# Selective scan: the product with C as one instruction per group on GpSimd, the product with B split unevenly between VectorE and GpSimd

## The chip, the cores and the metric

The kernel runs on one core of a Trainium2 chip. The metric is the device time of one execution in microseconds; the time of a kernel is the median of several executions. The core has five engines that work side by side, each through its own queue in order: TensorE (PE in the profile) multiplies matrices, VectorE (DVE) and GpSimd (POOL) work elementwise, ScalarE (ACT) applies functions such as exp, and SyncE (SP) here issues the transfers (DMA). They wait for each other through semaphores.

## The reference, cut to what matters

The program is a chain of four layers on an input of 2 images, 128 channels, 64 x 64 pixels: an attention layer, a layer of deformable convolutions, a layer of residual convolutions, and a layer of four selective scans. Only the last is touched. For each image, each of four directions (by rows forward and backward, by columns forward and backward) is a sequence of 4096 steps with 256 inner channels d and 16 states n:

```
dt  = softplus(dt @ W_dt.T + b_dt)
dA  = exp(dt[..., None] * A)                       # decay
dBu = dt[..., None] * Bm[:, :, None, :] * xh[..., None]
def step(h, inp):
    dA_t, dBu_t = inp
    h = dA_t * h + dBu_t
    return (h, h)
_, hs = lax.scan(step, h0, (dA.transpose(1, 0, 2, 3), dBu.transpose(1, 0, 2, 3)))
y = jnp.einsum('lbdn,bln->bld', hs, Cm)            # product with C, sum over n
y = y + xh * Dp
y = y * jax.nn.silu(z)
```

The four directions' results are joined, projected and added to the input.

## The kernel before, in words

Layer 3 is the function `layer3` (from line 1103). A sequence is cut into blocks of BLK = 512 steps: 2 images x 4 directions x 8 blocks make 64 blocks. In each block the 256 channels are two halves (`hf`), and the 16 states are four sets of four (`ng`). A half and a set make a group, so that a block has eight groups, numbered in this text 0 to 7 (4 x hf + ng), and the loop runs over 512 groups. In a group the 128 partitions hold 4 states x 32 channels, and four parts (`q`) of 512 steps each hold the half's four sets of 32 channels. The work of a group k:

- `weights` (line 1347): a matmul spreads the four rows of B over the partitions, into PSUM (tile `pbc`).
- `db_dve` (line 1361, VectorE) multiplies this B with dt times u (tile `dd4`, its second plane) for the first ND = 3 of the four parts; `db_pool` (line 1368, GpSimd) does the fourth, with a copy of B that a DMA has spread in SBUF[...]. Both write the tile `db`, of which there are four buffers.
- `expo` (line 1375, ScalarE): exp for the decay, one part at a time, into a PSUM tile `da` of which there are three; it runs two parts ahead of the scan.
- `scan` (line 1384, VectorE): one scan instruction for each part, in place in `db`.
- `keep` (line 1390, ScalarE) saves the last column of two parts to start the next block from.
- `cmul` (line 1395, GpSimd) multiplies two parts with C (also a copy spread by DMA), in place.
- `sums` (lines 1401 and 1403, PE) adds over the states into PSUM; after group 3 and group 7 of a block, `gate` (line 1412, VectorE) multiplies the sum with silu(z).

The order of all this is written out by hand in the loop that starts at line 1544; every engine takes its instructions in this order. In iteration k, VectorE has the four scans of group k, sometimes a gate, then `db_dve` of group k+1. GpSimd has `db_pool` of k+1, the second half of `cmul` of k-1, then the first half of `cmul` of k. ScalarE runs the decays, and between them the front work of the next block, spread over the iterations of the present one (`front_act`): in iteration 0 the silu that makes u, between two loads of its function table; 1 copies; 2 and 3 softplus; 4 a copy and `finish`; 5 the silu of z, again between two table loads. GpSimd has two small products of the next block's delta work in iterations 3 and 4 (`spread`). PE has that front work's matmuls ahead of `sums`. `transfers` puts the DMAs into SP's queue: storing and spreading delta (`spread_store`, `spread_load`, lines 1331 and 1340) and the copies of B and C (`copies`, line 1355).

Of the kernel before, what the change touches and what calls it, by code (L numbers as in the profile page):

```python
# [20 lines left out]
P = 128  # L21
# [3 lines left out]
BLK = 512  # L25
# [1077 lines left out]
def layer3(g, I, out):  # L1103
# [4 lines left out]

    nc, tc = g.nc, g.tc
    NJ = 4  # L1110
    ND = 3
    NNG = N_STATE // NJ
    HB = 3
    with ExitStack() as ctx:
# [66 lines left out]
        hl = a.tile([P, 2, NNG, 4, 1], F32, name="hl")  # L1181
# [58 lines left out]
        S = {}  # L1240
# [15 lines left out]
        def conv(i, hf):  # L1256
            blk = blocks[i]
            sgn = -1 if dirs[blk[1]][2] else 1
            pu = S[i]["pu", hf] = psm.tile([P, BLK], F32, name="pm3")
            for s in range(4):  # L1260
                nc.tensor.matmul(shaped(blk, pu), wcs[:, hf, s, :], window(blk, sgn * s), start=(s == 0), stop=(s == 3))  # L1261
# [33 lines left out]
        def bc_store(i):  # L1295
            S[i]["bx"] = dr.tile([2 * N_STATE, BLK], F32, name="bx")
            nc.sync.dma_start(S[i]["bx"], S[i]["xd"][: 2 * N_STATE])
# [30 lines left out]
        def spread_store(i, hf):  # L1328

            S[i]["dx", hf] = dr.tile([P, 2, BLK], F32, name="dx")  # L1330
            nc.sync.dma_start(S[i]["dx", hf], S[i].pop(("dd", hf)))

        def spread_load(i, hf):
            s_ = S[i]
            dx = s_.pop(("dx", hf))
            dd4 = d4.tile([P, 2, 4, BLK], F32, name="dd4")
            for x in range(2):
                src = dx[:, x, :].rearrange("(q c) t -> c q t", c=32)
                for j in range(NJ):
                    nc.sync.dma_start(dd4[32 * j : 32 * j + 32, x], src)  # L1340
            s_["d4", hf] = dd4

        def weights(k):

            i, hf, ng = groups[k]
            pb = psb.tile([P, BLK], F32, name="pbc")
            nc.tensor.matmul(pb, sel[:, ng].rearrange("p j c -> p (j c)"), S[i]["bc"], start=True, stop=True)  # L1347
            G[k] = {"pb": pb}

        def copies(i, x, ng):  # L1350

            t = S[i][x, ng] = ck.tile([P, BLK], F32, name=f"{x}4_{ng}", bufs=1)
            r0 = NJ * ng + (N_STATE if x == "c" else 0)
            for j in range(NJ):
                nc.sync.dma_start(t[32 * j : 32 * j + 32], S[i]["bx"][r0 + j].partition_broadcast(32))

        def db_dve(k):
            i, hf, ng = groups[k]
            x, n = G[k], ND
            x["db"] = wk.tile([P, 4, BLK], F32, name="db")  # L1360
            nc.vector.tensor_tensor(  # L1361
                x["db"][:, :n, :], x.pop("pb").unsqueeze(1).to_broadcast([P, n, BLK]), S[i]["d4", hf][:, 1, :n, :], ALU.mult
            )

        def db_pool(k):
            i, hf, ng = groups[k]
            x, n = G[k], ND
            nc.gpsimd.tensor_tensor(  # L1368
                x["db"][:, n:, :], S[i]["b", ng].unsqueeze(1).to_broadcast([P, 4 - n, BLK]), S[i]["d4", hf][:, 1, n:, :], ALU.mult
            )  # L1370
# [12 lines left out]
            first = i % NBLK == 0  # L1383
            nc.vector.tensor_tensor_scan(d1, d0, d1, 0.0 if first else hl[:, hf, ng, q, :], ALU.mult, ALU.add)  # L1384

        def keep(k, h):
            i, hf, ng = groups[k]
            last = 0 if dirs[blocks[i][1]][2] else BLK - 1
            qs = slice(2 * h, 2 * h + 2)
            nc.scalar.copy(hl[:, hf, ng, qs], G[k]["db"][:, qs, last : last + 1])  # L1390

        def cmul(k, h):
            i, hf, ng = groups[k]
            v = G[k]["db"][:, 2 * h : 2 * h + 2, :]
            nc.gpsimd.tensor_mul(v, v, S[i]["c", ng].unsqueeze(1).to_broadcast([P, 2, BLK]))  # L1395

        def sums(k):
            i, hf, ng = groups[k]
# [10 lines left out]
        def gate(i, hf):  # L1409
            s_ = S[i]  # L1410
            gt = s_["gt", hf] = ck.tile([P, BLK], F32, name="gt")
            nc.vector.tensor_tensor(gt, s_.pop(("y", hf)), s_["z"][:, hf, :], ALU.mult)  # L1412
# [24 lines left out]
        G = {}  # L1437

        def begin(i):
            if i < NBK:  # L1440
                S[i] = {}
                if i % (4 * NBLK) == 0:
                    columns_halo(blocks[i][0])
                if i % (4 * NBLK) == 2 * NBLK:
                    rows_halo(blocks[i][0])
                conv(i, 0)
# [3 lines left out]
        def front_act(i, slot):  # L1450
            if i < NBK:
                if slot == 0:
                    conv_silu(i)
                elif slot == 1:
                    xproj_copy(i)
                elif slot == 2:
                    softplus(i, 0)
                elif slot == 3:
                    softplus(i, 1)
                elif slot == 4:  # L1460
                    rest_copy(i)
                elif slot == 5:
                    zproj_silu(i)
# [18 lines left out]
        def front_pe(i, slot):  # L1482
            if i < NBK:
                if slot == 1:
                    xproj(i)
                elif slot == 2:
                    delta(i, 0)
                elif slot == 3:
                    delta(i, 1)
                elif slot == 4:  # L1490
                    xproj_rest(i)
                elif slot == 5:
                    zproj(i)
            if i + 1 < NBK:
                if slot == 6:
                    begin(i + 1)
                elif slot == 7:
                    conv(i + 1, 1)

        def front_pool(i, slot):  # L1500
            if i < NBK:
                if slot in (3, 4):
                    spread(i, slot - 3)
# [11 lines left out]
        with tc.manual_schedule():  # L1515
            tc.keep_in_program_order(nc.scalar.preload_act_table_set("natural_log_exp_and_others"))
            nc.scalar.activation(am, am, AF.Exp)
            nc.vector.tensor_scalar(am, am, -1.0, None, ALU.mult)
            for t in range(NBLK + 1):
                for s in LN:  # L1520
                    if 0 <= t - s // 8 < NBLK:
                        LN[s](0, t - s // 8)
            begin(0)
            conv(0, 1)
            for slot in range(8):
                front_pe(0, slot)
                front_act(0, slot)
                front_pool(0, slot)
            bc_store(0)
            for hf in range(2):  # L1530
                spread_store(0, hf)
            spread_load(0, 0)
            for ng in range(NNG):
                copies(0, "b", ng)
                copies(0, "c", ng)
            weights(0)
            weights(1)
            db_dve(0)
            db_pool(0)
            units = [(k, q) for k in range(len(groups)) for q in range(4)]  # L1540
            AHEAD = 2
            for u in range(AHEAD):
                expo(*units[u])
            for k in range(len(groups) + 6):
                i, slot = divmod(k, 8)
                live = k < len(groups)
                more = k + 1 < len(groups)
                ended = 1 <= k <= len(groups)
                transfers(i + 1, slot)
                if k + 2 < len(groups):  # L1550
                    weights(k + 2)
                for q in range(4):
                    if 4 * k + q + AHEAD < len(units):
                        expo(*units[4 * k + q + AHEAD])
                    if q == 0 and ended:
                        keep(k - 1, 1)
                    if live:
                        scan(k, q)

                    for j, hf in (((k - 5) // 8, 0), ((k - 9) // 8, 1)):  # L1560
                        if q == 3 and 8 * j + 5 + 4 * hf == k and 0 <= j < NBK:
                            gate(j, hf)

                    if q == 2 and live:
                        keep(k, 0)
                if more:
                    db_dve(k + 1)
                    db_pool(k + 1)
                if ended:
                    cmul(k - 1, 1)  # L1570
                front_pe(i + 1, slot)
                front_act(i + 1, slot)
                front_pool(i + 1, slot)
                if i >= 1 and i <= NBK:
                    if slot == 3:
                        project(i - 1)
                    elif slot == 4:
                        finish(i - 1)
                if live:
                    next_norm(i, slot)  # L1580
                if live:
                    cmul(k, 0)
                if ended:
                    sums(k - 1)

# [159 lines left out]
```

## Time and profile before

| | |
|---|---|
| median of 3 runs | 6007.57 us (5999.1 to 6009.02) |
| the profiled execution's own time | 6003.65 us |
| its span | 6001.9 us |
| busy in the span: PE | 5221.0 us (87%) |
| VectorE | 4554.2 us (76%) |
| ScalarE | 3807.3 us (63%) |
| GpSimd | 3701.6 us (62%) |
| first scan, last scan of layer 3 start at | 2554.8 us, 5990.1 us |

Shares over the whole span mix four layers. GpSimd is hardly used before 2500 us and almost without a pause after it, so the stage has to be read by itself. In a row of the profile's groups stand: line, engine, operation, tile written and tiles read, shapes and count; then the busy time in us and the mean ns of one; then the idle time of the engine just before these instructions, and what ended most of it.

### The profile page before, as it was taken

The numbers are of one execution on the slowest core, as the hardware profiler recorded it, in microseconds if no ns is written. First come the engines' busy times: TensorE is split into PE (matmuls) and PEld (weight loads), VectorE is DVE, ScalarE is ACT, GpSimd is POOL, SyncE is SP. The second block draws the span as 40 slices with busy tenths as digits, with TensorE's granted clock in tenths as the row PEclk, the third lists the DMA queues.
The fourth block names the chain that finished last, engine by engine and source line by source line (L and its number), as shares of the span: only waits on it lengthen the run. The fifth ranks groups of instructions, "written<-read, shape, count | busy, mean of one in ns | idle before, by whom it ended". The sixth has DMA issues, their size and how long they took to land.

```text
span 6001.9 us, 60094 instructions
## 1 busy us (share of the span) xinstructions
PE 5221.0 (87%) x18726; PEld 1662.7 (28%) x18726; DVE 4554.2 (76%) x4262; ACT 3807.3 (63%) x5867; POOL 3701.6 (62%) x2108
## 2 busy tenths in 40 slices
PE   6999999989978689888998888888898888887877
PEld 3333333334444334212222222222222222222221
DVE  5333333355134698499999999999999999999999
ACT  3888888840035411377777766777777777777765
POOL 5111111100010121199999999999999999999999
PEclk9999999999988899888888888888888888888887
DMA  5000001020066200165665556655665556655564
GB/s 152 18 18 18 18 18 32 1 58 1 15 111 110 51 7 0 28 144 135 145 144 133 138 134 145 143 131 135 150 145 132 141 132 145 145 134 137 135 151 106
DMA packets 373049, 575.61 MB, mean 96 GB/s; under 512 B 91080, under 2 KB 145744, under 8 KB 371632
## 3 DMA queue, kind: packets, MB, share of 16 engines
q1 hardware_dynamic: 367408, 563.94, 40.6%
q10 hardware_dynamic: 5312, 7.76, 0.5%
q8 instruction: 149, 2.44, 0.2%
q14 instruction: 180, 1.47, 0.1%
HBM read 482.34 MB, written 89.13 MB: 95 GB/s over the span
## 4 chain that ended last, share of the span: by engine, by line
DVE 45%; PE 38%; DMA 4%; issue 4%; POOL 4%; ACT 2%; SPq 2%; DVEq 0%; ACTq 0%; POOLq 0%
DVE db L1384 31%; DVE db L1361 11%; PE ps L269 10%; PE acc L285 8%; PE m L1034 5%; PE m L548 4%; DMA dd<-dx 2%; POOL db L1395 2%; PE acd L794 2%; PE pm L1261 1%; PE m L508 1%; DVE gt L1412 1%; PE pf L757 1%; PE py L1403 1%; PE pc L645 1%
## 5 line engine op out<-in xcount | busy, mean ns | idle before, releaser
L1395 POOL TENSOR_TENSOR db<-db,c 128x1024 f32<-128x1024 f32 x1024 | 2401.0, 2360 | 80.7 <-ACT hl L1390 67.5
L1384 DVE TENSOR_TENSOR_SCAN db<-da,hl,db 128x512 f32<-128x512 f32 x1792 | 2158.2, 1265 | 53.8 <-ACT da L1375 7.3
L1375 ACT ACTIVATE da<-dd,am 128x512 f32<-128x512 f32 x2048 | 1406.7, 689 | 918.0 <-DVE db L1384 904.0
L275 ACT ACTIVATE e<-ps 128x1024 f16<-128x1024 f32 x1024 | 992.3, 1021 | 134.8 <-PE ps L269 117.7
L1403 PE MATMUL py<-db,fold 128*32 128x512 f32 x4096 | 831.0, 686 | 203.4 <-POOL db L1395 202.9
L1361 DVE TENSOR_TENSOR db<-pbc,dd 128x1536 f32<-128x1536 f32 x512 | 888.2, 1735 | 51.1 <-DMA c<-bx 51.1
L1261 PE MATMUL pm<-xn,wcs 128*128 128x512 f32 x1024 | 722.8, 857 | 30.6 <-DVE xc L1199 17.6
L296 DVE RECIPROCAL rec<-acc 32x512 f32<-32x512 f32 x64 | 214.9, 3358 | 639.6 <-PE acc L285 612.1
L303 POOL TENSOR_TENSOR parts<-parts 32x512 f32<-32x512 f32 x64 | 80.6, 1259 | 975.3 <-DVE parts L302 975.3
L1368 POOL TENSOR_TENSOR db<-b,dd 128x512 f32<-128x512 f32 x512 | 651.2, 1272 | 21.1 <-DMA c<-bx 14.9
L269 PE MATMUL ps<-q,k 32*128 32x512 f32 x4096 | 656.4, 643 | 3.6 <-DVE flag L232 2.8
L285 PE MATMUL acc<-e,v 128*128 128x512 f16 x2048 | 531.3, 382 | 0.0
L1034 PE MATMUL m<-v,u 128*128 128x512 f32 x864 | 376.4, 598 | 51.6 <-DVE v L1003 51.6
L1401 PE MATMUL py<-u,ddp 128*128 128x512 f32 x256 | 183.6, 806 | 232.1 <-DVE gt L1412 231.8
L1347 PE MATMUL pbc<-bc,sel 64*128 64x512 f32 x512 | 284.2, 555 | 83.7 <-DVE db L1361 77.5
L1403 PEld LDWEIGHTS py<-db,fold 128*32 128x32 f32 x4096 | 115.1, 113 | 805.2 <-POOL db L1395 517.5
L1261 PEld LDWEIGHTS pm<-xn,wcs 128*128 128x128 f32 x1024 | 203.6, 209 | 428.8 <-issue 375.8
L1384 DVE TENSOR_TENSOR_SCAN db<-da,db 128x512 f32<-128x512 f32 x256 | 293.3, 1205 | 9.0 <-ACT da L1375 0.7
L285 PEld LDWEIGHTS <-v 128*128 128x128 bf16 x2048 | 158.5, 97 | 510.0 <-issue 388.7
L269 PEld LDWEIGHTS ps<-q,k 32*128 32x128 f32 x4096 | 229.7, 183 | 228.0 <-issue 147.2
L1347 PEld LDWEIGHTS pbc<-bc,sel 64*128 64x128 f32 x512 | 104.8, 205 | 607.6 <-DVE db L1361 306.3
L548 PE MATMUL m<-comb,w 64*128 64x512 f32 (+4 forms) x1296 | 269.9, 575 | 0.0
(311 smaller groups left out, 5734.9 us busy)
## 6 DMA issues: line engine op xcount, KB each, us to landing
dd<-dx SPq DMA_DIRECT2D x1024, 256.0 KB, 6.6
dx<-dd SPq DMA_DIRECT2D x128, 512.0 KB, 7.2
b<-bx SPq DMA_DIRECT2D x1024, 64.0 KB, 5.3
c<-bx SPq DMA_DIRECT2D x1024, 64.0 KB, 2.1
hats<-pos SPq DMA_DIRECT2D x136, 256.0 KB, 9.8
q<-qd SPq DMA_DIRECT2D x32, 512.0 KB, 8.6
w<-in_conv0T SPq DMA_DIRECT2D x18, 288.0 KB, 8.8
xa<-in_x SPq DMA_DIRECT2D x8, 512.0 KB, 9.1
```

Of the source, the lines that this page charges most:

```text
L269: nc.tensor.matmul(ps[:, i, :], k4[h % 2][rows, kb // 4, :], q4[h % 2][rows, qb * BLK : (qb + 1) * BLK], start=True, stop=True,)
L275: nc.scalar.activation(e[:, :n, :], ps[:, :n, :], AF.Exp)
L285: nc.tensor.matmul(acc, v3[b][:, kb, h, :], e[:, i, :], start=(kb == 0), stop=(kb == NS - 1))
L548: yield lambda q=q, dy=dy, src=src, i0=i0, i1=i1: nc.tensor.matmul(m[:, i0 * NF : i1 * NF], w[half, dy, q, x, :], src, start=(dy == KC and ...
L1034: nc.tensor.matmul(m[x], weights[j][:, dy, x, :], v[j][b][:, x, r0 : r0 + RP, :].rearrange("p r i -> p (r i)"), start=(dy == 0), stop=(dy ...
L1261: nc.tensor.matmul(shaped(blk, pu), wcs[:, hf, s, :], window(blk, sgn * s), start=(s == 0), stop=(s == 3))
L1361: nc.vector.tensor_tensor(x["db"][:, :n, :], x.pop("pb").unsqueeze(1).to_broadcast([P, n, BLK]), S[i]["d4", hf][:, 1, :n, :], ALU.mult)
L1368: nc.gpsimd.tensor_tensor(x["db"][:, n:, :], S[i]["b", ng].unsqueeze(1).to_broadcast([P, 4 - n, BLK]), S[i]["d4", hf][:, 1, n:, :], ALU.mult)
L1375: nc.scalar.activation(da, S[i]["d4", hf][:, 0, q, :], AF.Exp, scale=am[:, hf, q, ng : ng + 1])
L1384: nc.vector.tensor_tensor_scan(d1, d0, d1, 0.0 if first else hl[:, hf, ng, q, :], ALU.mult, ALU.add)
L1395: nc.gpsimd.tensor_mul(v, v, S[i]["c", ng].unsqueeze(1).to_broadcast([P, 2, BLK]))
L1403: nc.tensor.matmul(S[i]["y", hf][32 * q : 32 * q + 32, :], fold, G[k]["db"][:, q, :], start=False, stop=(ng == NNG - 1),)
```

## The change

The number of parts that VectorE multiplies with B now depends on half and set: (2, 4, 2, 4) in the first half, (2, 4, 1, 4) in the second. Where VectorE has all four, `db_pool` issues nothing, and the spread copies of B for sets 1 and 3 are no longer transferred. GpSimd's product with C is one instruction for the four parts of a group. It stands where the second half stood, one iteration after the group's scans; the first half at the end of the group's own iteration is gone. The last columns are likewise saved in one copy for the four parts, where the second copy stood.

```diff
@@ layer3 @@
-    ND = 3
+
+    ND = ((2, 4, 2, 4), (2, 4, 1, 4))
...
         def copies(i, x, ng):
 
+            if x == "b" and ND[0][ng] == ND[1][ng] == 4:
+                return
             t = S[i][x, ng] = ck.tile([P, BLK], F32, name=f"{x}4_{ng}", bufs=1)
...
         def db_dve(k):
             i, hf, ng = groups[k]
-            x, n = G[k], ND
+            x, n = G[k], ND[hf][ng]
...
         def db_pool(k):
             i, hf, ng = groups[k]
-            x, n = G[k], ND
+            x, n = G[k], ND[hf][ng]
+            if n == 4:
+                return
...
-        def keep(k, h):
+        def keep(k):
             i, hf, ng = groups[k]
             last = 0 if dirs[blocks[i][1]][2] else BLK - 1
-            qs = slice(2 * h, 2 * h + 2)
-            nc.scalar.copy(hl[:, hf, ng, qs], G[k]["db"][:, qs, last : last + 1])
-
-        def cmul(k, h):
+            nc.scalar.copy(hl[:, hf, ng], G[k]["db"][:, :, last : last + 1])
+
+        def cmul(k):
             i, hf, ng = groups[k]
-            v = G[k]["db"][:, 2 * h : 2 * h + 2, :]
-            nc.gpsimd.tensor_mul(v, v, S[i]["c", ng].unsqueeze(1).to_broadcast([P, 2, BLK]))
+            v = G[k]["db"]
+            nc.gpsimd.tensor_mul(v, v, S[i]["c", ng].unsqueeze(1).to_broadcast([P, 4, BLK]))
...
                     if q == 0 and ended:
-                        keep(k - 1, 1)
+                        keep(k - 1)
                     if live:
                         scan(k, q)
...
-                    if q == 2 and live:
-                        keep(k, 0)
                 if more:
                     db_dve(k + 1)
                     db_pool(k + 1)
                 if ended:
-                    cmul(k - 1, 1)
+                    cmul(k - 1)
...
                 if live:
                     next_norm(i, slot)
-                if live:
-                    cmul(k, 0)
                 if ended:
                     sums(k - 1)
```

## The prediction

> **What bounds the kernel now.** I read the busy times by stage first. The scan of layer 3 runs from 2554.8 to 5991.4 us, 64 blocks of 53.7 us. Two of its stretches (columns: length, then busy us of PE, weight loads, VectorE, ScalarE and GpSimd, then clock, DMA share, GB/s):
>
> ```profile
> 3000.00:3500.00 500.00, 435.74 (x1080) 105.80 (x1079) 492.04 (x394) 357.71 (x640) 487.73 (x266) 0.86 0.58 138
> 4500.00:5000.00 500.00, 440.87 (x1066) 102.68 (x1066) 491.80 (x393) 356.41 (x638) 485.62 (x262) 0.88 0.57 136
> ```
>
> VectorE is busy 98.4%, GpSimd 97%. The groups of the page give the pieces:
>
> ```profile
> L1395 POOL TENSOR_TENSOR db<-db,c 128x1024 f32<-128x1024 f32 x1024 | 2401.0, 2360 | 80.7 <-ACT hl L1390 67.5
> L1384 DVE TENSOR_TENSOR_SCAN db<-da,hl,db 128x512 f32<-128x512 f32 x1792 | 2158.2, 1265 | 53.8 <-ACT da L1375 7.3
> L1361 DVE TENSOR_TENSOR db<-pbc,dd 128x1536 f32<-128x1536 f32 x512 | 888.2, 1735 | 51.1 <-DMA c<-bx 51.1
> L1368 POOL TENSOR_TENSOR db<-b,dd 128x512 f32<-128x512 f32 x512 | 651.2, 1272 | 21.1 <-DMA c<-bx 14.9
> ```
>
> GpSimd's idle time is mostly for the copy of last columns (line 1390); VectorE's 51.1 us is one wait, before the first group. What VectorE waits for inside the scan stands in the waits by engine:
>
> ```profile
> DVE db L1384 <- ACT da L1375: 8.0, 11, 3.2
> ```
>
> Eight us in all. VectorE therefore sets the block time; whatever it saves counts, and whatever makes it wait costs. To see what is close behind, I follow one block in the timeline. I number a block's groups 0 to 7 (half hf, then ng) and call iteration s the loop pass with group s's scans. VectorE, around iterations 5 and 6 (start, duration, instruction):
>
> ```profile
> 3604.19 4.81 DVE L1384 TENSOR_TENSOR_SCAN db<-da,hl,db 128x512 f32<-128x512 f32 x4
> 3608.92 0.66 DVE L1412 TENSOR_TENSOR gt<-py,z 128x512 f32<-128x512 f32 x1
> 3609.50 1.75 DVE L1361 TENSOR_TENSOR db<-pbc,dd 128x1536 f32<-128x1536 f32 x1
> 3611.35 4.81 DVE L1384 TENSOR_TENSOR_SCAN db<-da,hl,db 128x512 f32<-128x512 f32 x4
> ```
>
> A scan takes 1.18 us from start to start; product and gap before the next scan take 1.85. ScalarE in the same time:
>
> ```profile
> 3607.86 0.69 ACT L1375 ACTIVATE da<-dd,am 128x512 f32<-128x512 f32 x1 [0.37 <-DVE db L1384]
> 3608.57 1.28 ACT L1279 ACT_TABLE_LOAD   x1
> 3609.86 1.09 ACT L1279 ACTIVATE z<-pm 128x512 f32<-128x512 f32 x2
> 3610.97 1.28 ACT L1280 ACT_TABLE_LOAD   x1
> 3612.26 0.69 ACT L1375 ACTIVATE da<-dd,am 128x512 f32<-128x512 f32 x1
> ```
>
> The decay of group 6's third scan waits behind the block of z work and is ready at 3612.95; about 0.05 us later a scan can use it, at 3613.00. VectorE gets there at 3611.35 + 2 x 1.18 = 3613.71. The margin is 0.71 us. I measured it so in 57 blocks: 0.70 to 0.72 in 50, 0.54 to 0.65 in 7. The same reading after the u work in iteration 0 gives a margin of about -0.07 in most blocks: there VectorE already loses 0.07 us.
>
> **What the Trainium skill says.** "Perfetto Trace Analysis", Tensor Engine Instruction: ScalarE, VectorE and GpSimd run strictly in order. The trace agrees: the decay above starts when the table load ends. "ScalarE: Activation LUTs", What ACT_TABLE_LOAD costs: a load takes about 1283 ns whatever the set; the trace shows 1283, so this block of work cannot shrink. "VectorE: DVE Perf Modes", The DRAIN you can't avoid: a same-engine read after write needs a semaphore; here 0.11 us pass between each product and its first scan, and the number of such pairs stays. Price: "GPSIMD Engine Reference", 3.1, gives 4497 ns on GpSimd and 2293 on VectorE for a two-input fp32 tensor_tensor of 2048 elements.
>
> **The change part by part** (per block, then x64).
>
> *Products with B on VectorE.* Before 8 x 3 = 24 parts; after 2+4+2+4+2+4+1+4 = 23, in the same eight instructions. The gate row (512 elements, also PSUM x SBUF) has 665 ns, the 1536-element row 1735: 535 a part and 130 fixed. So 1, 2 and 4 parts cost 0.665, 1.20 and 2.27 us. Saved: 0.535 x 64 = 34.2 us. With the page's 2293 for 2048 the saving is 6 us less; 6 either way goes into the range.
>
> *Cover taken from ScalarE.* In iteration 5 VectorE goes on to group 6, which has one part: it reaches the third scan 1.735 - 0.665 = 1.07 us earlier. Of that 0.71 is margin, 0.36 becomes a wait. ScalarE's block starts by the end of scan (5,2) and does not move. Over 63 blocks with z work: 55 x 0.36 + 8 x 0.45 (the smaller margins of a direction's first blocks) = 23.4 us lost. Group 1 gets four parts, which adds 0.535 in iteration 0 and removes that wait: 45 x 0.07, and 3 us of longer waits on decays in the trace: 6 us gained. Iteration 3 (second softplus) leads to group 4 with two parts: margin 1.45 falls to 0.92; a few blocks had 0.0 to 0.6, for which I add 1 us. Iteration 1: 3.53 falls to 3.0; iteration 7: at least 0.96 falls to 0.43.
>
> *GpSimd.* The 1024 product takes 2.33 us from start to start, the 512 one 1.23: 1.10 a part. Whole product with C: 1.10 x 4 + 0.13 = 4.53 (page: 4.50; two halves now: 4.66). Products with B: three of two parts (2.33) and one of three (3.42), 10.4 against 8 x 1.23 = 9.8. Before 8 x 4.66 + 9.8 + 5.2 (delta work) = 52.3; after 36.2 + 10.4 + 5.2 = 51.8 of a block of some 53.5. It stays under VectorE. Its whole product can now start only after the last scan and the copy. Walking through its queue from the start of a block, with ScalarE's copies at their present distance from the scans: product 0 may start at 9.06 us, ends 13.6; product 1 18.1; B-product for group 4, then product 2 21.2 to 25.7; delta work 28.3; product 3 32.9; delta 35.4; the three-part B-product 38.9; product 4 43.4, product 5 47.9; B-product for the next group 0 50.2; product 6 54.8, product 7 59.3 = 5.8 of the next block; B-product 8.1, before 9.06. So it catches up once a block. Who waits for it: scan (6,1) for the three-part product, due at 41.2, 2.4 us after; the gates after product 3 and 7, 4.7 and 5 us after PE's sums; the db buffers (four), over 5 us. No wait reaches VectorE. PE's z matmuls, behind sum 3, end at 36.8, ScalarE wants them at 38.25.
>
> *Copies of B for ng 1 and 3.* 512 transfers of 64 KB and 0.43 us of the SP queue each go. SP's waits are for delta work (853.9 us), and VectorE waits for no such transfer: 0. If this cover were gone, the relief could only help. Delta work ends 2 us later in the block (28.3 against 26.3); stored and loaded as now, its half lands at about 44.5, wanted at 47.9.
>
> *Copies of last columns* (line 1390): 512 fewer of 0.18 us on a ScalarE that waits 0.37 us beside them: 0.
>
> *The end.* The last product with C is 4.53 instead of 2.33 us after the last scan: +2.2, and some 0.3 for the sums: +2.5.
>
> Sum: -34.2 + 23.4 - 6 + 1 + 2.5 = -13.3 us. The profiled execution took 6003.65 (span 6001.9): 5990.4. The median of the three runs is 6007.57; the same difference gives **5994 us**.
>
> **Rivals.**
> *A, the gain comes whole:* ScalarE is ready for the third scan. For: the margin of 0.71 is read with a start latency seen only in the u case. Against: it is the same in 50 blocks. -34.2 - 6 + 2.5 = -38 us: 5970.
> *B, slower: GpSimd becomes the bound.* Place: the whole product with C, a form that the trace doesn't show. It decides from (53.5 - 15.6) / 8 = 4.74 us each. At 4.80 a block takes 54.0, 0.5 more: +32 on the forecast, 6026. For: two halves take 4.66 already. Against: the slope of the two forms and the page.
> *C, no difference:* GpSimd's product 3 ends over 1.4 us later than in my walk, PE's z matmuls follow, and ScalarE's block moves right: each us is a us of VectorE's wait. At 0.2 us a block the gain is gone: 6007. For: PE's clock is 0.83 to 0.88 and ScalarE already waits for PE in iteration 4. Against: margins of 1.4 us.
>
> **Chances.** Forecast 0.60, A 0.10, B 0.12, C 0.18. A measurement of this kernel tells about 0.2% (12 us) from no change. The forecast's own range is 5985 to 6003, its centre barely beyond that bound: 0.36 of its 0.60 faster, 0.24 the same. With A: faster 0.46. C with 0.01 of B: same 0.42, a little of C counting as slower; slower 0.12. The range takes in A and C, and B up to 4.78 us a product: 5968 to 6015.
>
> **What would show it.** Products of VectorE at 0.67, 1.20 and 2.27 us; GpSimd's at 4.53; a wait of VectorE for the decay (line of the exponent) once a block, before group 6's third scan, some 0.36 us each and 23 in all; none in iteration 0; block time 53.5 us. Wrong it would be if GpSimd is busy over 99% or VectorE waits on products of GpSimd or on gates.

## The result, and the profile after

The changed kernel takes 6044.84 us (median; 6041.86 to 6050.66) against 6005.65 us for the kernel before: ratio 1.0068, 95% interval 1.005 to 1.0085. It is slower by 39 us where 12 to 13 us less was forecast. The profiled execution's span is 6040.1 us, 38.2 more than before.

The groups of the page for the four kinds of instruction that were shown of before:

```profile
L1399 POOL TENSOR_TENSOR db<-db,c 128x2048 f32<-128x2048 f32 x512 | 2311.0, 4528 | 58.5 <-ACT hl L1394 57.9
L1389 DVE TENSOR_TENSOR_SCAN db<-da,hl,db 128x512 f32<-128x512 f32 x1792 | 2162.7, 1265 | 113.2 <-ACT da L1380 66.3
L1364 DVE TENSOR_TENSOR db<-pbc,dd 128x2048 f32<-128x2048 f32 (+2 forms) x512 | 854.8, 1670 | 51.1 <-DMA c<-bx 51.1
L1373 POOL TENSOR_TENSOR db<-b,dd 128x1024 f32<-128x1024 f32 (+1 forms) x256 | 673.7, 2632 | 136.2 <-DMA c<-bx 86.6
```

The instructions cost what was expected: 4528 ns for the whole product with C, and VectorE's products are 33 us shorter in all (888.2 to 854.8). The time went into waits: the idle time before the scans rose from 54 to 113 us. The busy times of the same two stretches of the scan, columns as before:

```profile
3000.00:3500.00 500.00, 406.01 (x1054) 102.93 (x1056) 476.89 (x386) 339.84 (x550) 471.55 (x149) 0.84 0.52 125
4500.00:5000.00 500.00, 421.89 (x1039) 103.47 (x1043) 472.22 (x380) 336.31 (x542) 462.79 (x145) 0.83 0.53 125
```

VectorE falls from 98.4% to about 95%, GpSimd from 97% to 93 or 94%: neither is busy throughout, so neither sets the block time by its work alone. The waits by engine, over the scan of layer 3 (from 2554 us on), name the next link, VectorE's first, then ScalarE's:

```profile
DVE db L1389 <- ACT da L1380: 76.3, 93, 3.7
```

```profile
ACT u L1267 <- PE pm L1262: 72.6, 30, 4.1
```

VectorE waits 76 us for the decay, in 93 places. In 63 of them it waits before group 6's third scan, as forecast, 17 us in all (23 forecast); in the other 30 before group 1's third scan, 59 us, which the prediction does not have. ScalarE waits 72.6 us in 30 places for line 1262, a convolution of the next block's front work. Before, this was 3.6 us.

**Where the blocks differ.** I took the time from one start of group 0's product on VectorE to the next. In the row directions (blocks 16 to 31 and 48 to 63) an ordinary block takes 53.50 us (53.74 before), as forecast. In the column directions (0 to 15 and 32 to 47) the median is 55.17. By classes of these distances, after minus before: 30 of column directions +50.4 us, 24 of row directions -5.4, the 8 with layer norm (in which the second image is normalized) -5.4, the first -0.2. They sum to 39.4 us. The rest of the 38.2 us between the two spans lies outside: the first of these products starts 5.5 us earlier, after layers that the change doesn't touch, and from the last one to the end 4.4 us more pass. VectorE's timeline in a row block:

```profile
3626.80 0.67 DVE L1416 TENSOR_TENSOR gt<-py,z 128x512 f32<-128x512 f32 x1
3627.38 0.68 DVE L1364 TENSOR_TENSOR db<-pbc,dd 128x512 f32<-128x512 f32 x1
3628.17 2.46 DVE L1389 TENSOR_TENSOR_SCAN db<-da,hl,db 128x512 f32<-128x512 f32 x2
3630.87 2.46 DVE L1389 TENSOR_TENSOR_SCAN db<-da,hl,db 128x512 f32<-128x512 f32 x2 [0.25 <-ACT da L1380]
```

That is the forecast wait before group 6's third scan. In a column block there is another, in iteration 1, before group 1's third scan (VectorE, then ScalarE, then PE, then GpSimd, all around the same block's end):

```profile
2774.48 2.46 DVE L1389 TENSOR_TENSOR_SCAN db<-da,hl,db 128x512 f32<-128x512 f32 x2
2778.48 2.46 DVE L1389 TENSOR_TENSOR_SCAN db<-da,hl,db 128x512 f32<-128x512 f32 x2 [1.54 <-ACT da L1380]
```

```profile
2773.06 0.69 ACT L1267 ACTIVATE u<-pm,vecs 128x512 f32<-128x512 f32 x1
2775.75 0.69 ACT L1267 ACTIVATE u<-pm,vecs 128x512 f32<-128x512 f32 x1 [2.01 <-PE pm L1262]
2776.46 1.28 ACT L1268 ACT_TABLE_LOAD   x1
2777.76 0.69 ACT L1380 ACTIVATE da<-dd,am 128x512 f32<-128x512 f32 x1
```

```profile
2757.45 1.93 PE L1407 MATMUL py<-db,fold 128*32 128x512 f32 x8 [3.06 <-POOL db L1399]
2759.31 0.79 PE L1348 MATMUL pbc<-bc,sel 64*128 64x512 f32 x1
2760.04 7.21 PE L1262 MATMUL pm<-xn,wcs 128*128 128x512 f32 x8
2767.18 1.06 PE L1407 MATMUL py<-db,fold 128*32 128x512 f32 x8
2768.18 0.49 PE L1348 MATMUL pbc<-bc,sel 64*128 64x512 f32 x1
2768.60 7.12 PE L1262 MATMUL pm<-xn,wcs 128*128 128x512 f32 x8
```

```profile
2752.89 9.01 POOL L1399 TENSOR_TENSOR db<-db,c 128x2048 f32<-128x2048 f32 x2
2776.88 2.36 POOL L1373 TENSOR_TENSOR db<-b,dd 128x1024 f32<-128x1024 f32 x1 [3.63 <-DMA c<-bx]
```

Read backwards: the third scan waits for a decay, which stands behind the u work; u's second half waits for the second convolution, which ends at about 2775.7; the two convolutions take 7.1 us each and stand in PE's queue behind the sums of group 4, which wait until GpSimd has ended product 4 with C at 2757.40. Before, in the same block, these sums began 2.7 us earlier, and the second convolution ended 2.7 us earlier, though the next block began at nearly the same time (2766.24 us then, 2766.09 now):

```profile
2754.74 2.21 PE L1403 MATMUL py<-db,fold 128*32 128x512 f32 x8
2756.89 0.63 PE L1347 MATMUL pbc<-bc,sel 64*128 64x512 f32 x1
2757.45 7.12 PE L1261 MATMUL pm<-xn,wcs 128*128 128x512 f32 x8
2764.49 1.06 PE L1403 MATMUL py<-db,fold 128*32 128x512 f32 x8
2765.49 0.49 PE L1347 MATMUL pbc<-bc,sel 64*128 64x512 f32 x1
2765.91 7.12 PE L1261 MATMUL pm<-xn,wcs 128*128 128x512 f32 x8
```

The first theory from this: a ring. GpSimd's late products delay the convolutions, and the sums of group 6 behind the second convolution release the buffer that GpSimd needs for group 2 (the 3.63 us above, which the profile puts down to a transfer). There are two rivals: PE is merely late, and nothing comes back to GpSimd (the one-way theory); or the transfer that the profile names is late (the transfer theory).

### The profile page after: what moved, and what is told of

Same layout as the page of the kernel before. It is cut to its first block, busy times and chain, and to the rows that moved or that the text cites. A ratio compares the mean times of both kernels' runs of the same rounds, so it can differ in the third digit from the quotient of the medians.

```text
span 6040.1 us, 57348 instructions
## 1 busy us (share of the span) xinstructions
PE 5093.3 (84%) x18726; PEld 1660.5 (27%) x18726; DVE 4525.1 (75%) x4262; ACT 3749.8 (62%) x5355; POOL 3658.3 (61%) x1340
## 4 chain that ended last, share of the span: by engine, by line
PE 46%; DVE 27%; POOL 12%; ACT 5%; issue 5%; DMA 4%; SPq 1%; DVEq 0%; POOLq 0%; ACTq 0%
DVE db L1389 19%; PE ps L269 10%; PE acc L285 8%; PE pm L1262 7%; DVE db L1364 7%; POOL db L1399 7%; PE m L1034 5%; PE m L548 4%; POOL db L1373 2%; PE py L1407 2%; PE acd L794 2%; ACT da L1380 1%; PE m L508 1%; POOL dd L1326 1%; DMA dd<-dx 1%
## 5 line engine op out<-in xcount | busy, mean ns | idle before, releaser
L1399 POOL TENSOR_TENSOR db<-db,c 128x2048 f32<-128x2048 f32 x512 | 2311.0, 4528 | 58.5 <-ACT hl L1394 57.9
L1407 PE MATMUL py<-db,fold 128*32 128x512 f32 x4096 | 671.8, 734 | 479.9 <-POOL db L1399 478.3
L1364 DVE TENSOR_TENSOR db<-pbc,dd 128x2048 f32<-128x2048 f32 (+2 forms) x512 | 854.8, 1670 | 51.1 <-DMA c<-bx 51.1
L1373 POOL TENSOR_TENSOR db<-b,dd 128x1024 f32<-128x1024 f32 (+1 forms) x256 | 673.7, 2632 | 136.2 <-DMA c<-bx 86.6
L1262 PE MATMUL pm<-xn,wcs 128*128 128x512 f32 x1024 | 736.3, 871 | 8.4 <-ACT xn L1215 4.8
L1407 PEld LDWEIGHTS py<-db,fold 128*32 128x32 f32 x4096 | 86.2, 116 | 927.0 <-POOL db L1399 709.5
L1262 PEld LDWEIGHTS pm<-xn,wcs 128*128 128x128 f32 x1024 | 220.0, 227 | 412.8 <-issue 378.2
L1405 PE MATMUL py<-u,ddp 128*128 128x512 f32 x256 | 166.6, 736 | 192.0 <-DVE gt L1416 191.7
L1348 PE MATMUL pbc<-bc,sel 64*128 64x512 f32 x512 | 300.0, 586 | 31.8 <-DVE db L1364 31.4
```

The costliest lines, as they stand in the source:

```text
L1364: nc.vector.tensor_tensor(x["db"][:, :n, :], x.pop("pb").unsqueeze(1).to_broadcast([P, n, BLK]), S[i]["d4", hf][:, 1, :n, :], ALU.mult)
L1373: nc.gpsimd.tensor_tensor(x["db"][:, n:, :], S[i]["b", ng].unsqueeze(1).to_broadcast([P, 4 - n, BLK]), S[i]["d4", hf][:, 1, n:, :], ALU.mult)
L1407: nc.tensor.matmul(S[i]["y", hf][32 * q : 32 * q + 32, :], fold, G[k]["db"][:, q, :], start=False, stop=(ng == NNG - 1),)
```

## The experiments

All ratios are to the kernel before, run on the same chip. The last two columns are medians of ordinary column and row blocks in us: blocks with layer norm and the first blocks of a direction are left out.

| run | time us | ratio, 95% interval | column | row |
|---|---|---|---|---|
| before | 6005.65 | 1 | 53.74 | 53.74 |
| the change | 6044.84 | 1.0068 (1.005 to 1.0085) | 55.17 | 53.50 |
| products with B alone | 5988.49 | 0.997 (0.996 to 0.9981) | 53.50 | 53.50 |
| whole product with C alone | 6040.25 | 1.0059 (1.0042 to 1.0075) | 54.61 | 53.75 |
| change, convolution by rows | 5979.91 | 0.996 (0.9946 to 0.9974) | 53.50 | 53.50 |
| change, sums 6 first | 6137.38 | 1.0222 (1.0205 to 1.0239) | 56.92 | 55.28 |
| change, five buffers | 6037.1 | 1.0051 (1.0034 to 1.0068) | 55.06 | 53.50 |
| change, one-part group moved | 6012.9 | 1.0011 (1.0004 to 1.0018) | 54.09 | 53.15 |
| change, convolutions early | 5994.57 | 0.998 (0.9971 to 0.9988) | 53.55 | 53.50 |
| halves, one-part group moved | 5965.49 | 0.9933 (0.9916 to 0.995) | 53.15 | 53.15 |
| whole alone, convolutions early | 6042.7 | 1.0061 (1.0044 to 1.0077) | 54.63 | 53.75 |
| change, early and moved | 6013.69 | 1.0016 (1.0009 to 1.0022) | 54.47 | 53.15 |
| whole alone, by rows | 6012.88 | 1.0013 (1.0006 to 1.002) | 53.75 | 53.75 |
| before, by rows | 6000.84 | 0.9992 (0.9984 to 1.0001) | 53.74 | 53.74 |

**The two parts alone.**

```diff
-    ND = 3
+    ND = ((2, 4, 2, 4), (2, 4, 1, 4))      # keep and cmul stay in halves
```

> The uneven products with B alone; the product with C and the copies of last columns in halves as before. Ring theory: the ring holds two, two and three parts of products with B (8.1 us against 6.2) but the first half of product 0 is ahead of it again: about 53.4 us in column blocks, just under VectorE's 53.5; with the wait before group 6's third scan left, 5985 to 5995. One-way theory: product 4 ends about 1.9 us later than before through the parts of group 6, ScalarE's u work waits about 0.5 us in the column blocks: about 6005. Transfer theory: the transfers are those of the changed kernel, so 6045 or little less.

5988.49: the products with B alone bring 16 us, a little more than was forecast for the whole change; the block time is 53.50 in both directions. The transfers dropped are the same as in the change, so they are not what costs.

```diff
-    ND = ((2, 4, 2, 4), (2, 4, 1, 4))
+    ND = ((3, 3, 3, 3), (3, 3, 3, 3))      # keep and cmul as changed
```

> The whole product with C (and one copy of last columns) alone; VectorE has three parts of every group as before. Ring theory: the ring takes about 52.3 us, under VectorE's 53.7: no wait, only the longer end, about 6008. One-way theory: the whole product 4 ends as late as in the changed kernel less 2.2 us, waits of under 0.5 us in column blocks, 6005 to 6020. Transfer theory: as before, 6006.

6040.25, a miss for every theory: the whole product alone costs 35 us. By the profiled executions 21 us of them lie in the 30 column blocks, which take 54.61 us; 3 lie in the first block, 4 in row blocks, 4 at the end, 2 elsewhere. So for the column blocks the ring had been summed too short.

**The length of the convolution.**

```diff
-                nc.tensor.matmul(shaped(blk, pu), wcs[:, hf, s, :], window(blk, sgn * s), start=(s == 0), stop=(s == 3))
+                nc.tensor.matmul(pu, wcs[:, hf, s, :], flat(xns[blk[0]])[:, HB * HW + blk[2] * BLK - sgn * s : HB * HW + (blk[2] + 1) * BLK - sgn * s], start=(s == 0), stop=(s == 3))
```

> The changed kernel, but the convolution reads its input in row order in every direction, so that the column directions compute another convolution: this leaves out the strided reading, nothing else. Ring and one-way theory: a convolution takes 3.7 us everywhere, the waits in iteration 1 go, all blocks 53.5 us, about 5990. Transfer theory: no difference, 6045.

5979.91, 65 us under the change, and the waits in iteration 1 are gone; of the 62.7 us between the profiled executions 57.6 lie in the column blocks. The groups of the lines, over 2700 to 3400 us, a stretch of column blocks, show what the edit moved; first the change, then this run:

```profile
L1262 PE MATMUL pm<-xn,wcs 128*128 128x512 f32 x208 | 180.4, 1022 | 0.4 <-POOL xn L1230 0.4
```

```profile
L1262 PE MATMUL pm<-xn,wcs 128*128 128x512 f32 x219 | 116.0, 676 | 0.4 <-POOL xn L1230 0.4
```

**Cutting the ring at the sums.**

```diff
                     cmul(k - 1)
+                if ended and slot == 7:
+                    sums(k - 1)
                 front_pe(i + 1, slot)
...
-                if ended:
+                if ended and slot != 7:
                     sums(k - 1)
```

> The changed kernel, with only PE's order in iteration 7 altered: the sums of group 6 stand before the second convolution of the next block instead of behind it. Ring theory: in the column blocks PE's two convolutions (7.1 us each) and GpSimd's products form a ring that takes 55.1 us, because GpSimd's product with B for group 2 waits for the buffer that these sums release; with the sums first the ring is cut, GpSimd's wait of 3.6 us in iteration 1 goes, all blocks come to 53.5 us, and the time is about 5990 (0.25% under before, some 55 us under the changed kernel). One-way theory (PE is merely late because GpSimd's product 4 ends later): the second convolution starts 1.1 us later still, the wait in iteration 1 grows by about 1 us in 31 blocks, 6075. Transfer theory (GpSimd waits for a late copy, as the profile names it): no difference, 6045.

6137.38. The ring theory in this form fell: GpSimd's wait for the buffer did vanish, but VectorE's wait more than doubled.

```profile
DVE db L1389 <- ACT da L1380: 168.6, 116, 6.9
```

The second convolution now waits for product 6 too, also in row blocks. What counts is when that convolution ends. From there I walked on by hand, with the rows shown and those of softplus, starting where a second convolution ends: u, table load, decay 2.8 us; group 1's last two scans, gate and product 4.3; group 2's first three scans, decay, softplus, decay, copy of last columns 7.6; in all 14.7. Then product 2 may start: three whole products 13.5, delta work 5.2, three-part product with B 3.4, in all 22.1. Then PE from the end of product 4: 18.25 to the end of the second convolution. That closes a **loop** of 55.05 us: 14.7 + 22.1 + 18.25. Beside it stands the one through the buffer, 55.2: from the end of the second convolution 1.2 to the product with B for group 2, 13.6 for it, products 0 and 1 and the next product with B, then the same 22.1 and 18.25. With the whole product alone, where VectorE has one part with B more on this way and GpSimd one fewer, the same sum gives 54.7 (measured 54.61). With halves only the second half of product 2 has to wait for the copy: 53.1 with the uneven split, 52.8 in the kernel before, both under VectorE's 53.5 and 53.7. For a fifth buffer the two ways round predict different things:

```diff
-        wk = ctx.enter_context(tc.tile_pool(name="l3wk", bufs=4))
+        wk = ctx.enter_context(tc.tile_pool(name="l3wk", bufs=5))
...
-        sel = a.tile([4 * N_STATE, 2 * NNG, NJ, 32], F32R, name="sel")
+        sel = a.tile([4 * N_STATE, NNG, NJ, 32], F32R, name="sel")
...
```

> The changed kernel with five db buffers instead of four (the room comes from a constant table, half of which is never read), so that the product with B for group 2 need not wait for the sums of group 6. Buffer theory: that wait of 3.6 us closes the ring; without it column blocks come to 53.5 us, about 5990. Loop theory: from the end of the second convolution there is a second way round of nearly the same length, u work, decay, VectorE's scans, softplus, copy of last columns of group 2, products 2, 3 and 4 with C (14.5 + 22.2 us), then PE's 18.3 us of sums and convolutions: 55.0 us against 55.2. So the wait goes and the time hardly moves: 6035 to 6045.

6037.1, column blocks 55.06. GpSimd's timeline in this run shows the wait change its place: the product with B for group 2 starts at once, and the next product with C waits for the copy of last columns instead, which ScalarE does after the late u work.

```profile
2776.55 2.40 POOL L1373 TENSOR_TENSOR db<-b,dd 128x1024 f32<-128x1024 f32 x1
2782.03 8.99 POOL L1399 TENSOR_TENSOR db<-db,c 128x2048 f32<-128x2048 f32 x2 [3.08 <-ACT hl L1394]
```

That the wait goes with a fifth buffer shows also that it was for a buffer, not for the transfer that the profile names. The trace of the change agrees: 29 of its 30 such waits end 0.17 us after PE's sums end, whatever the profile names.

**The size of the loop.**

```diff
-    ND = ((2, 4, 2, 4), (2, 4, 1, 4))
+    ND = ((1, 4, 2, 4), (2, 4, 2, 4))
```

> The changed kernel with the one-part group moved: (1, 4, 2, 4), (2, 4, 2, 4) instead of (2, 4, 2, 4), (2, 4, 1, 4). Loop theory: GpSimd has two parts instead of three between product 3 and product 4, the loop is 1.1 us shorter, 54.1 us in column blocks; and the wait before group 6's third scan goes, as 1.07 us less cover becomes 0.54 less, under the margin of 0.71: 53.2 us in row blocks. About 5995 to 6005. Buffer theory: the same 54.1. If neither place matters: 6045.

Column blocks 54.09, row blocks 53.15, as summed; the time, 6012.9, lies above the range. The trace, of the fastest of its executions (6007.56), shows further waits in layer-norm blocks and near the end; what made the others longer is open.

**Opening the loop.**

```diff
-                front_pe(i + 1, slot)
+                early = not 21 <= i <= 31
+                if early and slot == 6 and i + 2 < NBK:
+                    conv(i + 2, 1)
+                elif not (early and slot == 7):
+                    front_pe(i + 1, slot)
+                if early and slot == 5 and i + 2 < NBK:
+                    begin(i + 2)
```

> The changed kernel with PE's order altered outside the blocks with layer norm: the first convolution of the next block stands in iteration 5, ahead of the sums of group 4, the second in iteration 6, ahead of the sums of group 5. Loop theory: the convolutions no longer wait for product 4, the loop is open, all blocks take 53.5 us: 5980 to 5990. One-way theory: the same. If the stall came from PE's total load, which is unchanged: 6045.

5994.57, 50 us under the change with the same instructions: column blocks 53.55. That is 4.6 us above the range, which I did not follow up. PE's load didn't change, only what its convolutions stand behind.

> The whole product with C alone (VectorE three parts of every group, as in the run that lost 35 us) with the convolutions ahead of the sums as in the run before. Loop theory: the 35 us were the closed loop, so with it open column blocks are back at 53.7 us and the time is that of before within some 5 us: 6000 to 6012. If the whole product costs by itself: 6040.

6042.7, a miss. In this order the sums of group 5 stand behind the second convolution, and with three parts everywhere GpSimd has a product with B for group 1, which needs group 5's buffer. GpSimd's waits:

```profile
POOL db L1373 <- DVE db L1389: 72.5, 27, 3.0
```

They lie in iteration 0 of 27 column blocks, 2.7 us each. The profile names VectorE's scans, but 25 of them end 0.17 us after PE's sums end, as the buffer waits above did. ScalarE then waits for PE in iterations 2 and 5. In the run before, group 1 had no such product. That this is the cause is read from the trace, not tried. The run doesn't tell what the whole product costs by itself; the next pair does.

> The whole product with C alone, with the convolution reading in row order in every direction (the column directions compute another convolution). Loop theory: the loop is some 6.8 us shorter in the column blocks, 47.8 us, far under VectorE's 53.74; the 35 us go, and the time is that of before in row order within 5 us (longer end). If the whole product costs by itself, or by GpSimd's load: 6035 to 6040.

> The kernel before with the convolution reading in row order in every direction (the column directions compute another convolution): the control for the two runs in row order. Loop theory: the loop of before takes about 52.7 us in column blocks, already under VectorE's 53.74, so nothing is gained but waits at the change of direction: 5998 to 6006.

6012.88 and 6000.84, column blocks 53.75 and 53.74: with the short convolution the whole product alone loses 12 us to its control instead of 35, and nothing in an ordinary block. Within 5 us was expected. Of the 11.8 us between the profiled executions 3.6 lie ahead of the first group's product, 2.1 in the first block, some 4 in the other blocks, where waits of 0.3 us lie scattered, and 2.1 at the end. Before gains next to nothing from the short convolution: its loop was open already.

**Better versions.**

> Products with C in halves as before, products with B as (1, 4, 2, 4), (2, 4, 2, 4). Both theories: the loop takes about 52 us, VectorE's block is 53.17 us without the wait before group 6: 0.33 us a block less than the run with the split alone (5988.5), and some 8 us of waits on GpSimd in the layer-norm blocks less: 5960 to 5970.

5965.49, faster than before by 0.67% (0.5 to 0.84%): the products with B split unevenly, the one part at group 0, where no ScalarE work follows, and the product with C left in halves. VectorE's wait for decays is all but gone:

```profile
DVE db L1388 <- ACT da L1379: 4.3, 4, 2.5
```

> The changed kernel with both repairs: convolutions ahead of the sums, and the one-part group at group 0. Loop theory: 53.2 us in all ordinary blocks, 0.33 us under the run with the order alone (5994.6): 5970 to 5978. It may be slower than the split in halves with the shift (5965.5) by the longer end and the layer-norm blocks.

6013.69, a miss by 36 us: with the one part at group 0, GpSimd has three parts for it, into group 4's buffer, whose sums the early order puts behind the first convolution. Its trace has 25 us of GpSimd's waits that the profile puts down to those sums, in iteration 7; counting all that end 0.17 us after PE's sums there are 35, with 56 us. Its ordinary column blocks lie mostly near 53.5 or near 54.6, so that their median says little. Read, not tried.

## Why the prediction was wrong

Right, point by point. *Products with B on VectorE*: forms of 0.68, 1.20 and 2.27 us, and the part alone brought 16 us where this sum, with what follows from it, gave 13 to 16. *Cover taken from ScalarE*: the wait before group 6's third scan appears in all 63 blocks, in most of them 0.25 us of idle, with a block of 53.50 where 53.5 was summed; moving the one part took it away and 0.35 us a block with it. The wait in iteration 0 went in row blocks. *GpSimd*: 4528 ns for the whole product ("GPSIMD Engine Reference", 3.1, in the Trainium skill: 4497), the queue in row blocks to within a few tenths of the walk. *Copies of B*: nothing (SP's waits for delta work are 881.4 us over the scan of before, not the 853.9 that I read; nothing hangs on it). *The end*: the last gate waits 6.93 us instead of 3.83, +3.1 against +2.5.

The step that failed is "No wait reaches VectorE" in the part on GpSimd. The walk listed who waits for GpSimd: a scan, the gates, the buffers, PE's z matmuls. It left out the work behind the sums of groups 4 and 5 in PE's queue, the next block's two convolutions, and their taker, ScalarE's u work. And it was made in one block between 3570 and 3680 us, a row block, where a convolution takes 3.7 us; in column blocks it takes 7.1, and half of all blocks are such. This one term was put at nothing, and it is the error: these 30 blocks took 50.4 us more where the forecast, 0.25 us a block, makes 7.5 less, 58 us apart. The forecast and the change in the span are 51.5 apart, mainly because the layers ahead happened to take 5.5 us less in the profiled execution. Of the signs of being wrong that I had named, neither came: GpSimd is not over 99% busy, and VectorE's waits show as waits for decays, as in the forecast.

*Rival C* had the mechanism, GpSimd late, PE late, ScalarE's block moved, but at product 3 and the z matmuls; it happened at product 4 and u. *Rival B*, GpSimd as the bound, didn't happen: GpSimd is less busy than before. *The one-part group* was seen as ScalarE's trouble only; its three parts on GpSimd stand right ahead of product 4, and moving them takes 1.1 us off the loop. On *the whole product*, the 2.2 us that it adds between the copy of last columns and all that follows were booked at the end of the kernel; inside, they lengthen the loop once a block. The margins were all taken as one-way slacks. In a loop a delay comes back after one turn, and the test is whether the turn is shorter than the block: 52.8 against 53.7 before, 55.1 against 53.5 after.

"SBUF — State Buffer" in the Trainium skill, under Door 1: The DMA port swizzle, says that each access that crosses to a new 16-byte line pays a penalty; it gives no size for a matmul. The column windows read such a pattern. That these 16-byte lines cause the difference is not shown here. The trace of before held the number all along: 7.12 us for the eight matmuls of a column block, shown above, against 3.70 in a row block:

```profile
3613.95 3.70 PE L1261 MATMUL pm<-xn,wcs 128*128 128x512 f32 x8
```

## What to carry to other kernels

Before judging a queue's delay by margins, follow everything behind the delayed instruction on its engine, and its takers, until the path comes back to where it started; if it does, add up the turn and compare it with the time that one block takes on its busiest engine. Do this once for each kind of iteration: the same line can cost twice as much where a view is read across rows. And when two edits share such a turn, their costs don't add: here -16 and +35 made +39.

## What the runs showed of the hardware that was not expected

A matmul whose 512 fp32 columns are read with a stride of 64 elements takes 0.86 us from start to start, against 0.43 for contiguous ones (7.12 and 3.70 us for eight), at the same instruction shape and at a granted clock of 1.00 in both places. A wait for a tile buffer was shown in the profile as one for a transfer, in another run as one for VectorE's scans. A fifth buffer told them apart, and so does the distance of 0.17 us from the end of PE's sums to the start of GpSimd's product.
